# Layer 0 of a four-layer network: score tiles in PSUM banks of their own, single banks for the rest, and two convolutions as matrix products

## The chip, the cores and the metric

The kernel runs on one core of one Trainium2 chip. The metric is the time of one execution on the device in microseconds; the time before is a median of three executions, 4436.91 us (4435.02 to 4451.55). One more execution was profiled. A core has five engines that work side by side: TensorE (PE in the profile, its weight loads PEld), VectorE (DVE), ScalarE (ACT), GpSimd (POOL) and SyncE (SP), which issues most DMAs. TensorE writes into PSUM only, here eight banks of 512 fp32 numbers per partition; ScalarE and VectorE read the banks.

## The reference, cut to what matters

The input is eight samples of 256 channels by 32 x 32 points, fp32. Four layers follow one another. Only layer 0 is touched:

```python
def _attention(x, ...):
    qkv = _bn(_conv1x1(x, qkv_w), ...).reshape(B, NH, 2 * KD + HD, N)     # 4 heads, KD = 32, HD = 64, N = 1024
    attn = softmax(einsum('bhkn,bhkm->bhnm', q, k) * SCALE)
    out = einsum('bhdm,bhnm->bhdn', v, attn).reshape(B, Cc, H, W)
    out = out + _bn(_dwconv3(v_img, pe_w), ...)
    return _bn(_conv1x1(out, proj_w), ...)

def _edffn(x, pi_w, dw_w, fft_p, po_w):
    x = _conv1x1(x, pi_w)                  # 256 -> 1024 channels
    x = _dwconv3(x, dw_w)                  # 3 x 3, each channel by itself
    x1, x2 = x[:, :hid], x[:, hid:]
    x = gelu(x1) * x2
    x = _conv1x1(x, po_w)                  # 512 -> 256
    # patches of 8 x 8: rfft2, times fft_p, irfft2
    ...

x = x + gamma1 * _attention(_ln(x, norm1_w, norm1_b), ...)
x = x + gamma2 * _edffn(_ln(x, norm2_w, norm2_b), ...)
```

Layers 1 to 3 (a deformable convolution; an attention with a routed feed-forward; an attention with a mixture of experts) read what layer 0 wrote.

## The kernel before, in words

`fast0` is layer 0. It is written as generators: each `yield` ends a piece, and `by_time` merges the pieces of all streams by a time of their own, given at the end of `fast0` in units of half an attention step (`T = 32` units to a sample). The merged order is a priority; a planner then orders the instructions of each engine, by this priority and by when its own costs say that inputs and buffers are there. The order it finds is fixed in the program, each engine runs its list in order, and semaphores hold an instruction until its inputs and buffers are ready. Work of layer 1 (`net.head()`, and what follows it) is merged in behind layer 0's end, and the planner may place it earlier where an engine would be idle.

The streams of a sample `b`:

- `before_attention`: root-mean-square norm (`normed`: squares, `ms` as a product with `mean64`, `r`, then `rb`, which spreads `r` over the partitions, and `xn` = x times `rb` on VectorE), the products for v, q and k (`projected`), the transposes of v (`vT`), and the 3 x 3 position convolution (`pe`), for which `thrice` holds three shifted copies of v, loaded by DMA.
- `attention`: one stream for all samples, 8 x 2 x 8 = 128 steps. A step makes scores for four heads (`s`, four products of 512 columns, L1357), two exponentials of 1024 on ScalarE (`e`, L1363), and for the step before it the sums of `e` on VectorE (L1319) and the products with v (`A`, L1323). `finish` divides by the sums (`D`, `rr`, `av`), adds `o`, and makes the output product (`proj`), which VectorE adds to x (L1351).
- `before_gates` and `gates`: the second norm, then eight convolutions `convolved(i)` in the order 0, 1, 4, 5, 2, 3, 6, 7. Each is a product (`pi`, L78), its reading by ScalarE (`hp`, L1398), and `depthwise`: the middle tap on ScalarE (L1223) and eight taps on VectorE (L1230), each a multiply-add over the image. `hp` has two buffers. GELU and a product on VectorE (`gate`, L1409) follow, and `gated` goes to DRAM.
- `transforms`: four groups of patches: `po` (L1448), its copy `u` by ScalarE, the forward transform (`fwd`, L1455), a product with `gain` on VectorE (L1456), the transform back (`back`, L1463) and an addition to x on VectorE (L1469).

PSUM: `psS` has three pairs of banks for all tiles of `pair` and `bank`, scores among them; `psA` has one pair for `A`. `bank` takes a pair too and uses its first half. When the attention stream is done, `att.close()` gives up its buffers, and the rest of layer 0 (the last sample's gates, the transforms of the last two) runs with the head of layer 1, which has two banks of its own.

Of the kernel before, what the change touches and what calls it, by code (L numbers as in the profile page):

```python
# [17 lines left out]
P = 128  # L18
B = 8
# [1074 lines left out]
def fast0(net, io):  # L1094
    tc, nc = net.tc, net.nc
    NH, KD = 4, 32
    SCALE = KD ** (-0.5)
    NT = N // P
    yield HOLD
    with ExitStack() as ctx, ExitStack() as att:  # L1100
        wp = io.pool(ctx, "f0w", 1)
        one = io.pool(ctx, "f0a", 1)
        two = io.pool(ctx, "f0b", 2)
        five = io.pool(ctx, "f0e", 5)
        psS = io.pool(ctx, "f0s", 3, PSUM)

        awp = io.pool(att, "f0aw", 1)
        aone = io.pool(att, "f0aa", 1)
        atwo = io.pool(att, "f0ab", 2)
        afive = io.pool(att, "f0ae", 5)  # L1110
        psA = io.pool(att, "f0am", 1, PSUM)
        nc.scalar.preload_act_table_set("natural_log_exp_and_others")

        vec = net.load(wp, "f0_vec")
# [18 lines left out]
        pib = wp.tile([P, 8], F32, name="pib")  # L1133
        gain = net.load(wp, "l0_gam2")

        def pair(name):
            return psS.tile([P, 2, HF], F32, tag="S", name=name)

        def bank(name):
            return pair(name)[:, 0]  # L1140

        with ExitStack() as tmp:
            ini = io.pool(tmp, "f0i", 1)
# [54 lines left out]
        def normed(xn, x, sq):  # L1198

            ps = bank("ms")  # L1200
            for k in range(KC):
                s_ = sq(k)
                nc.scalar.activation(s_, x[:, k, :], AF.Square)
                for h in range(2):
                    nc.tensor.matmul(
                        ps[64 * h : 64 * h + 64], lhsT=net.mean64, rhs=s_[:, bass.ts(h, HF)],
                        start=(k == 0), stop=(k == KC - 1),
                    )
            r = one.tile([P, HF], F32, tag="r", name="r")
            net.rsqrt(r, ps, net.eps6)  # L1210
            yield
            pr = pair("rb")
            for h in range(2):
                nc.tensor.matmul(
                    pr[:, h], lhsT=net.unit[64 * h : 64 * h + 1, :], rhs=r[64 * h : 64 * h + 1, :],
                    start=True, stop=True,
                )
            pr = pr.rearrange("p h n -> p (h n)").unsqueeze(1).to_broadcast([P, KC, N])
            nc.vector.tensor_tensor(xn, x, pr, ALU.mult)  # L1219

        def depthwise(out, src, taps):

            nc.scalar.activation(out, src, AF.Identity, scale=taps(4))  # L1223
            for t_ in (0, 1, 2, 3, 5, 6, 7, 8):
# [6 lines left out]
                if t_ % 2:  # L1231
                    yield

        def before_attention(b):
            xn = aone.tile([P, KC, N], F32, tag="xn", name="xn")
            nc.sync.dma_start(out=xn, in_=io.src[b])
            yield
            v = aone.tile([P, KC, N], F32, tag="v", name="v")
            yield from normed(xn, xn, lambda k: v[:, k, :])
            yield  # L1240
            def projected(d, w, j, norm):
                ps = pair("qkv")
                for h in range(2):
                    net.linear(ps[:, h], w, xn, bass.ts(j, P), bass.ts(h, HF))
                nc.scalar.activation(d, ps.rearrange("p h n -> p (h n)"), AF.Identity, scale=sc(norm), bias=sh(norm))

            for c in range(KC):
                projected(v[:, c, :], wv, c, 2 + c)
                yield
            for d, (j, name) in ((qs, (0, "q")), (ks, (1, "k"))):  # L1250
                d[b] = atwo.tile([P, N], F32, tag=name, name=name)
                projected(d[b], wqk, j, j)
                yield

            va = vas[b] = atwo.tile([P, NT, KC, P], F32, tag="va", name="va")
            for t4 in range(0, NT, 4):
                ps = pair("vT")
                for i in range(4):
                    for c in range(KC):
                        lo = (i % 2) * C + c * P  # L1260
                        nc.tensor.transpose(ps[:, i // 2, lo : lo + P], v[:, c, bass.ts(t4 + i, P)], net.ident)
                nc.scalar.copy(
                    va[:, t4 : t4 + 4].rearrange("p t c d -> p (t c d)"), ps.rearrange("p h n -> p (h n)")
                )
                yield

            o = os[b] = atwo.tile([P, KC, N], F32, tag="o", name="o")
            for c in range(KC):
                ps = pair("pe")
                for h in range(2):  # L1270

                    thrice = aone.tile([96, 4, HF], F32, tag="thrice", name="thrice")
                    edge = thrice[0:32, :, :IMG] if h == 0 else thrice[64:96, :, HF - IMG :]
                    nc.gpsimd.memset(edge, 0.0)  # L1274
                    for j in range(3):
                        n = HF * h + IMG * (j - 1)
                        lo, hi = max(0, n), min(N, n + HF)
                        for g in range(4):
                            nc.sync.dma_start(
                                out=thrice[32 * j : 32 * j + 32, g, lo - n : hi - n],  # L1280
                                in_=v[32 * g : 32 * g + 32, c, lo:hi],
                            )
                    yield
                    for j, s_ in enumerate((0, -1, 1)):
                        for g in range(4):
                            to, fr = (
                                img(a)[:, :, max(0, -d_) : IMG - max(0, d_)]
                                for a, d_ in ((ps[32 * g : 32 * g + 32, h], s_), (thrice[:, g, :], -s_))
                            )
                            nc.tensor.matmul(  # L1290
                                to, lhsT=wpe[:96, c, s_ + 1, g, :], rhs=fr, start=(j == 0), stop=(j == 2)
                            )
                    yield
                nc.scalar.activation(
                    o[:, c, :], ps.rearrange("p h n -> p (h n)"), AF.Identity, scale=sc(4 + c), bias=sh(4 + c)
                )
                yield

        def attention():
# [31 lines left out]
            def finish(b, gq, A, total, x):  # L1331
# [13 lines left out]
                nc.vector.tensor_tensor(av, av, rr.unsqueeze(1).to_broadcast([P, KC, HF]), ALU.mult)  # L1345
                nc.vector.tensor_tensor(o[:, :, cols], o[:, :, cols], av, ALU.add)
                yield
                ps = pair("proj")
                for c in range(KC):
                    net.linear(ps[:, c], wproj, o, bass.ts(c, P), cols)  # L1350
                    nc.vector.scalar_tensor_tensor(x[:, c], ps[:, c], sh(6 + c), x[:, c], ALU.add, ALU.add)  # L1351
                nc.sync.dma_start(out=mids[b][:, :, cols], in_=x)

            for i, (b, gq, kt) in enumerate(steps):
                ss = [pair("s") for _ in range(2)]
                for h in range(NH):
                    nc.tensor.matmul(  # L1357
                        ss[h // 2][:, h % 2], lhsT=ks[b][32 * h : 32 * h + 32, bass.ts(kt, P)],
# [31 lines left out]
        def gates(b):  # L1390
            xn = xs.pop(b)

            def convolved(i):
                hp = two.tile([P, N], F32, tag="hp", name="hp")
                ps = pair("pi")
                for h in range(2):
                    net.linear(ps[:, h], wpi, xn, bass.ts(i, P), bass.ts(h, HF))
                nc.scalar.activation(hp, ps.rearrange("p h n -> p (h n)"), AF.Identity, bias=pib[:, i : i + 1])  # L1398
                a = cv[i] = five.tile([P, N], F32, tag="a", name="a")
                yield  # L1400
                yield from depthwise(img(a), img(hp), lambda t_: dw_taps[:, i, t_ : t_ + 1])

            cv, sts = {}, {}

# [23 lines left out]
        def transforms(b):  # L1428
# [12 lines left out]
            for pr in range(4):  # L1441
                hc, x = ahead.pop(pr)
                if pr < 3:
                    fetch(pr + 1)
                ps = pair("po")
                for pc in range(2):
                    for k in range(4):
                        nc.tensor.matmul(  # L1448
                            ps[:, 0, bass.ts(pc, C)], lhsT=hc[:, k, pc, :], rhs=wpo[:, k, :],
                            start=(k == 0), stop=(k == 3),  # L1450
                        )
                u = one.tile([P, 2, C], F32, tag="u", name="u")
                nc.scalar.copy(u.rearrange("p t c -> p (t c)"), ps[:, 0])
                yield
                nc.tensor.matmul(ps[:, 1], lhsT=fwd, rhs=u.rearrange("p t c -> p (t c)"), start=True, stop=True)  # L1455
                nc.vector.tensor_tensor(  # L1456
                    u, ps[:, 1].rearrange("p (t c) -> p t c", c=C), gain.unsqueeze(1).to_broadcast([P, 2, C]), ALU.mult
                )
                yield
                back = pair("back")  # L1460
                for c in range(KC):
                    for pc in range(2):
                        nc.tensor.matmul(  # L1463
                            back[:, 0, (2 * c + pc) * P : (2 * c + pc + 1) * P], lhsT=u[:, pc, bass.ts(c, P)],
                            rhs=inv, start=True, stop=True,
                        )
                for c in range(KC):
                    xt = x[:, c, :].rearrange("p (h q w) -> p q h w", q=2, w=16)
                    nc.vector.tensor_tensor(  # L1469
                        xt, back[:, 0, bass.ts(c, C)].rearrange("p (q h w) -> p q h w", q=2, w=16), xt, ALU.add  # L1470
                    )
                nc.sync.dma_start(out=io.dst[b][:, :, bass.ts(pr, C)], in_=x)
                yield
# [13 lines left out]
            next(streams[1][2])  # L1487
        rest = by_time(streams, until=main)
        att.close()
        by_time(rest + [[T * B + 1, 2, net.head()]])  # L1490


# [1657 lines left out]
```

## Time and profile before

| | |
|---|---|
| median of three executions | 4436.91 us (4435.02 to 4451.55) |
| the profiled execution, its span | 4446.59 us, 4444.7 us |
| PE busy over the span | 4017.9 us (90%) |
| DVE, ACT busy over the span | 2316.8 us (52%), 2146.1 us (48%) |
| mean granted TensorE clock | 0.952 |
| one tap of `depthwise` on VectorE (L1230) | 1232 ns, 512 of them |
| `pi`, 128x512 (L78) | 512 records, mean 629 ns |
| scores `s` (L1357), exponentials `e` (L1363) | 1024 records, mean 643 ns; 256, mean 1020 ns |

A product of fp32 numbers shows as two records of TensorE, so `pi` has 8 x 8 x 2 x 2 = 256 products and 512 records. [...]the pitch between records is what counts, 3.70 us for eight of `pi` in a row. "Idle before" is the idle time of an engine ahead of an instruction, and behind the arrow stands what ended it. Views of a stretch of time give microseconds from the start of the span.

### The profile page before, as it was taken

The numbers are of one execution on the slowest core, as the hardware profiler recorded it, in microseconds if no ns is written. First come the engines' busy times: TensorE is split into PE (matmuls) and PEld (weight loads), VectorE is DVE, ScalarE is ACT, GpSimd is POOL, SyncE is SP. The second block draws the span as 40 slices with busy tenths as digits, with TensorE's granted clock in tenths as the row PEclk, the third lists the DMA queues.
The fourth block names the chain that finished last, engine by engine and source line by source line (L and its number), as shares of the span: only waits on it lengthen the run. The fifth ranks groups of instructions, "written<-read, shape, count | busy, mean of one in ns | idle before, by whom it ended". The sixth has DMA issues, their size and how long they took to land. (4 is left out here: it accounts for less than half of the span.)

```text
span 4444.7 us, 52329 instructions
## 1 busy us (share of the span) xinstructions
PE 4017.9 (90%) x19836; PEld 1911.5 (43%) x19836; DVE 2316.8 (52%) x3935; ACT 2146.1 (48%) x2736; POOL 555.6 (13%) x634
## 2 busy tenths in 40 slices
PE   8989999999887899989999978888999999999887
PEld 3223333333333444444444435553333443336776
DVE  2387777777888677742222266622333223324355
ACT  3454445444443466634334364425555555566443
POOL 0000000000000000000000023330000000353753
PEclk9999999999998999999999989999999999999997
DMA  2212222222222111010001023362100000236666
GB/s 85 77 50 83 87 73 88 81 76 80 69 89 82 58 59 49 31 41 19 20 19 38 10 88 105 97 207 76 34 29 29 10 20 29 75 122 201 183 221 244
DMA packets 188423, 348.44 MB, mean 78 GB/s; under 512 B 23706, under 2 KB 132460, under 8 KB 176644
## 3 DMA queue, kind: packets, MB, share of 16 engines
q1 hardware_dynamic: 165396, 293.31, 20.4%
q0 software_dynamic: 19104, 46.45, 3.0%
q10 hardware_dynamic: 3664, 5.24, 0.3%
q8 instruction: 160, 2.62, 0.2%
q14 instruction: 99, 0.81, 0.1%
HBM read 174.24 MB, written 152.04 MB: 73 GB/s over the span
## 5 line engine op out<-in xcount | busy, mean ns | idle before, releaser
L1230 DVE SCALAR_TENSOR_TENSOR a<-hp,w_f_vec,a 128x992 f32<-128x992 f32 (+1 forms) x512 | 627.9, 1232 | 150.2 <-ACT a L1223 142.6
L2611 ACT ACTIVATE e<-s,five 128x1024 f32<-128x1024 f32 x512 | 539.3, 1110 | 274.2 <-PE s L2605 273.7
L2605 PE MATMUL s<-q,k 32*128 32x512 f32 x2048 | 368.5, 673 | 20.0 <-ACT e L2611 17.9
L1363 ACT ACTIVATE e<-s 128x1024 f32<-128x1024 f32 x256 | 249.6, 1020 | 229.0 <-PE s L1357 228.9
L2589 PE MATMUL A<-e,v 128*32 128x512 f32 x2048 | 296.9, 635 | 17.8 <-ACT e L2611 17.8
L1319 DVE TENSOR_TENSOR sum<-sum,e 128x1024 f32<-128x1024 f32 x192 | 230.7, 1219 | 115.9 <-ACT e L1363 115.9
L1323 PE MATMUL A<-e,va 128*32 128x512 f32 x2048 | 288.7, 602 | 0.0
L78 PE MATMUL pi<-xn,w_l_wpi 128*128 128x512 f32 x512 | 248.0, 629 | 36.9 <-ACT e L1363 20.0
L1357 PE MATMUL s<-q,k 32*128 32x512 f32 x1024 | 195.1, 643 | 12.8 <-DVE xn L1219 7.1
L2605 PEld LDWEIGHTS s<-q,k 32*128 32x128 f32 x2048 | 116.7, 191 | 202.5 <-issue 82.8
L1398 ACT ACTIVATE hp<-pi,pib 128x1024 f32<-128x1024 f32 x64 | 71.4, 1115 | 234.6 <-PE pi L78 228.7
L78 PEld LDWEIGHTS pi<-xn,w_l_wpi 128*128 128x128 f32 x512 | 97.8, 200 | 177.9 <-issue 110.4
L1681 PE MATMUL pos<-pos,w_f_sel 64*128 64x512 f32 x576 | 163.7, 633 | 5.4 <-ACT ay L1707 2.1
L2759 PE MATMUL h<-xk,w 128*128 128x128 f32 x1136 | 145.5, 283 | 20.4 <-DVE xk L2747 20.2
L1021 POOL DMA_INDIRECT res<-y,to x142 | 143.5, 1011 | 123.0 <-issue 87.3
L2730 ACT COPY w<-w_l3f_w 128x512 f32 x142 | 88.3, 624 | 144.1 <-PE h L2759 142.3
L2759 PEld LDWEIGHTS h<-xk,w 128*128 128x128 f32 x1136 | 142.1, 198 | 26.9 <-DVE xk L2747 20.2
L78 PE MATMUL h<-xk,w_l2f_w 128*128 128x512 f32 x256 | 125.5, 648 | 27.9 <-DVE xk L2136 27.9
L1274 POOL MEMSET thrice<- 32x128 f32 x32 | 6.3, 196 | 1117.4 <-PE pe L1290 1072.3
L1323 PEld LDWEIGHTS A<-e,va 128*32 128x32 f32 x2048 | 61.3, 109 | 193.8 <-issue 191.5
L2589 PEld LDWEIGHTS A<-e,v 128*32 128x32 f32 x2048 | 42.5, 110 | 234.2 <-issue 201.7
L1021 POOL DMA_INDIRECT so<-xl,rows x128 | 129.5, 1012 | 90.5 <-DMA xl<-mox 62.7
(397 smaller groups left out, 7032.9 us busy)
## 6 DMA issues: line engine op xcount, KB each, us to landing
x<-d SPq DMA_DIRECT2D x32, 1024.0 KB
xs<-so SPq DMA_DIRECT2D x70, 260.0 KB
so<-zero SPq DMA_DIRECT2D x5, 3380.0 KB
thrice<-v SPq DMA_DIRECT2D x256, 64.0 KB
gated<-st SPq DMA_DIRECT2D x32, 512.0 KB
hc<-gated SPq DMA_DIRECT2D x32, 512.0 KB
d<-x SPq DMA_DIRECT2D x16, 1024.0 KB
xl<-mox SPq DMA_DIRECT2D x64, 256.0 KB
```

What stands on the lines that cost most here:

```text
L78: self.nc.tensor.matmul(ps, lhsT=w[:, i, m], rhs=src[:, i, cols], start=(i == 0), stop=(i == k - 1))
L1021: made = self.nc.gpsimd.indirect_dma_start(**args)
L1230: nc.vector.scalar_tensor_tensor(to, fr, taps(t_), to, ALU.mult, ALU.add)
L1319: nc.vector.tensor_tensor(half, half, e[j], ALU.add)
L1323: nc.tensor.matmul(state["A"][32 * h : 32 * h + 32, c, :], lhsT=vas[b][:, kt, c, 32 * h : 32 * h + 32], rhs=e[h // 2][:, h % 2, :], start= ...
L1357: nc.tensor.matmul(ss[h // 2][:, h % 2], lhsT=ks[b][32 * h : 32 * h + 32, bass.ts(kt, P)], rhs=qs[b][32 * h : 32 * h + 32, bass.ts(gq, HF) ...
L1363: nc.scalar.activation(es[i][j], ss[j], AF.Exp, scale=SCALE)
L1681: nc.tensor.matmul(ps[:, bass.ts(h, HF)], lhsT=sel[r, t, xy, :], rhs=poss[b][r, :], start=True, stop=True)
L2589: nc.tensor.matmul(A[32 * h : 32 * h + 32], lhsT=v[:, kt, c * P + 32 * h : c * P + 32 * h + 32], rhs=e[:, h, :], start=first, stop=last,)
L2605: nc.tensor.matmul(ss[h // 2][:, h % 2], lhsT=k[32 * h : 32 * h + 32, c, bass.ts(kt, P)], rhs=q[32 * h : 32 * h + 32, c, bass.ts(hh, HF)], ...
L2611: nc.scalar.activation(e[:, 2 * j : 2 * j + 2], ss[j], AF.Square, scale=SCALE, bias=five)
L2759: nc.tensor.matmul(ps[:, j, m], lhsT=ws[j][:, k, bass.ts(m, P)], rhs=xk[:, j, k], start=(k == 0), stop=(k == KC - 1),)
```

## The change

- `psS` now has two pairs, and only scores use it. All other tiles take single banks `X`, of which there are two while attention runs: 4 + 2 + 2 (`psA`) is again eight. Tiles that were a pair (`pi`, `qkv`, `vT`, `pe`, `rb`, `proj`) become two banks, and ScalarE or VectorE reads each bank by an instruction of its own. `po` and `fwd`, which shared a pair, are two tiles. The tile of `pe` is taken after `thrice` is loaded, not before.
- After the attention stream `X` is a new pool of four banks.
- For the last sample, convolutions 1 and 7 go through `by_products`: ScalarE makes nine 128 x 128 matrices with the taps of a channel on the diagonal, and for each half of the image nine products with shifted windows add up in a bank, which ScalarE copies out.

```diff
+    BY_PRODUCTS, HROWS = (1, 7), IMG // 2
...
-        psS = io.pool(ctx, "f0s", 3, PSUM)
+        own = {"X": io.pool(ctx, "f0x", 2, PSUM)}
...
-        psA = io.pool(att, "f0am", 1, PSUM)
+        psS, psA = io.pool(att, "f0s", 2, PSUM), io.pool(att, "f0am", 1, PSUM)
...
-        def pair(name):
-            return psS.tile([P, 2, HF], F32, tag="S", name=name)
-
         def bank(name):
-            return pair(name)[:, 0]
+            return own["X"].tile([P, HF], F32, tag="X", name=name)
...
+        def by_products(out, src, i):
+
+            diag = own["diag"].tile([P, 9, P], F32, tag="dg", name="dg")
+            for t_ in range(9):
+                nc.scalar.activation(diag[:, t_], net.ident, AF.Identity, scale=dw_taps[:, i, t_ : t_ + 1])
+            for h in range(2):
+                ps = bank("dw")
+                for n, t_ in enumerate((4, 0, 1, 2, 3, 5, 6, 7, 8)):
+                    dy, dx = t_ // 3 - 1, t_ % 3 - 1
+                    lo, hi = max(0, HROWS * h + dy) - dy, min(IMG, HROWS * h + HROWS + dy) - dy
+                    x0, x1 = max(0, -dx), IMG - max(0, dx)
+                    nc.tensor.matmul(
+                        img(ps)[:, lo - HROWS * h : hi - HROWS * h, x0:x1], lhsT=diag[:, t_],
+                        rhs=img(src)[:, lo + dy : hi + dy, x0 + dx : x1 + dx], start=(n == 0), stop=(n == 8),
+                    )
+                    if n in (4, 8):
+                        yield
+                nc.scalar.copy(out[:, bass.ts(h, HF)], ps)
...
             def projected(d, w, j, norm):
-                ps = pair("qkv")
                 for h in range(2):
-                    net.linear(ps[:, h], w, xn, bass.ts(j, P), bass.ts(h, HF))
-                nc.scalar.activation(d, ps.rearrange("p h n -> p (h n)"), AF.Identity, scale=sc(norm), bias=sh(norm))
+                    ps = bank("qkv")
+                    net.linear(ps, w, xn, bass.ts(j, P), bass.ts(h, HF))
+                    nc.scalar.activation(d[:, bass.ts(h, HF)], ps, AF.Identity, scale=sc(norm), bias=sh(norm))
...
-                ps = pair("proj")
                 for c in range(KC):
-                    net.linear(ps[:, c], wproj, o, bass.ts(c, P), cols)
-                    nc.vector.scalar_tensor_tensor(x[:, c], ps[:, c], sh(6 + c), x[:, c], ALU.add, ALU.add)
+                    ps = bank("proj")
+                    net.linear(ps, wproj, o, bass.ts(c, P), cols)
+                    nc.vector.scalar_tensor_tensor(x[:, c], ps, sh(6 + c), x[:, c], ALU.add, ALU.add)
...
-                ss = [pair("s") for _ in range(2)]
+                ss = [psS.tile([P, 2, HF], F32, tag="S", name="s") for _ in range(2)]
...
-                ps = pair("pi")
                 for h in range(2):
-                    net.linear(ps[:, h], wpi, xn, bass.ts(i, P), bass.ts(h, HF))
-                nc.scalar.activation(hp, ps.rearrange("p h n -> p (h n)"), AF.Identity, bias=pib[:, i : i + 1])
+                    ps = bank("pi")
+                    net.linear(ps, wpi, xn, bass.ts(i, P), bass.ts(h, HF))
+                    nc.scalar.activation(hp[:, bass.ts(h, HF)], ps, AF.Identity, bias=pib[:, i : i + 1])
...
-                yield from depthwise(img(a), img(hp), lambda t_: dw_taps[:, i, t_ : t_ + 1])
+                if b == B - 1 and i in BY_PRODUCTS:
+                    yield from by_products(a, hp, i)
+                else:
+                    yield from depthwise(img(a), img(hp), lambda t_: dw_taps[:, i, t_ : t_ + 1])
...
         att.close()
+        own["X"], own["diag"] = io.pool(ctx, "f0t", 4, PSUM), io.pool(ctx, "f0d", 2)
```

`rb`, `vT`, `pe`, `po`, `fwd` and `back` are changed in the same way as `projected` and `proj`.

## The prediction

> **What bounds the kernel now.** I read the page's slices first, then a table of stretches, then the waits of the engine that is busiest in them, then the order of time where the stretches change. The slices (slice 12 ends at 1333 us) put layer 0 in the first 13: from the third on TensorE is at 80 to 90% and VectorE at 70 to 80%, and in slices 11 to 13 TensorE falls and VectorE rises.
>
> ```profile
> PE   8989999999887899989999978888999999999887
> DVE  2387777777888677742222266622333223324355
> ```
>
> The table of stretches, cut where the timeline shows attention's last step (1310), the last sample's normalised input (1358), its last convolution (1462) and layer 1's first `pos` product (1501):
>
> ```profile
> core 0: us, PE busy (x) PEld busy (x) DVE busy (x) ACT busy (x) POOL busy (x), PEclk, DMA share, GB/s
> 50.00:1310.00 1260.00, 1151.51 (x5644) 417.54 (x5641) 915.62 (x846) 589.42 (x629) 6.07 (x31) 0.97 0.24 74
> 1310.00:1358.00 48.00, 27.48 (x74) 9.89 (x74) 32.72 (x39) 16.10 (x23) 6.01 (x6) 0.69 0.46 168
> 1358.00:1462.00 104.00, 69.70 (x248) 35.40 (x244) 95.99 (x107) 34.89 (x43) 0.00 (x0) 0.86 0.18 62
> 1462.00:1501.00 39.00, 38.58 (x174) 21.52 (x168) 10.03 (x19) 4.74 (x9) 0.50 (x2) 0.97 0.36 116
> ```
>
> Up to 1310 TensorE sets the pace (1151.5 of 1260 us; idle 108.5). From 1358 VectorE does (96.0 of 104; TensorE idle 34.3). From 1462 TensorE is full again. What ends TensorE's idle time in 50 to 1310:
>
> ```profile
> PE pi L78 <- ACT e L1363: 20.0, 18, 1.1
> PE proj L78 <- DVE x L1351: 15.5, 9, 2.5
> PE pi L78 <- DVE xn L1219: 13.6, 7, 2.2
> PE qkv L78 <- DVE xc L1469: 9.3, 4, 2.3
> PE pe L1290 <- DMA thrice<-v: 9.1, 7, 2.1
> PE proj L78 <- ACT e L1363: 7.8, 7, 1.1
> PE s L1357 <- DVE xn L1219: 7.1, 5, 5.7
> PE proj L78 <- DVE o L1346: 5.4, 2, 4.2
> ...
> PE s L1357 <- ACT e L1363: 2.2, 2, 1.1
> ...
> PE s L1357 <- DVE u L1456: 1.5, 1, 1.5
> PE s L1357 <- DVE xc L1469: 1.2, 1, 1.2
> ```
>
> `pi` doesn't read `e`, and `s` reads none of `xn`, `u`, `xc`: these are waits for a pair of banks, not for data. The tail in order of time, VectorE's and TensorE's:
>
> ```profile
> 1411.07 11.57 DVE L1230 SCALAR_TENSOR_TENSOR a<-hp,w_f_vec,a 128x992 f32<-128x992 f32 x10
> ...
> 1447.46 0.58 PE L1548 MATMUL gn_m<-gn_mv,w_f_gsel 128*128 128x1 f32 x2 [11.48 <-DVE gn_mv L1545]
> 1456.02 0.59 PE L1557 MATMUL gn_v<-gn_t,w_f_gsel 128*128 128x1 f32 x2 [7.97 <-DVE gn_t L1554]
> ```
>
> VectorE adds one tap every 1.157 us, back to back, and TensorE has nothing to do for 20 us.
>
> [...]18 waits of `pi` for an exponential, none over 1.1 us. [...]the rows show 586 (`u`) and 1010 (`av`). [...]So the bank of an operation queued behind taps stays taken. `back` shows it: from its last matmul to the start of a reading addition 4.2 us pass on average, against 0.04 us (median) from `pi` to `hp`, which ScalarE reads.
>
> **The change part by part.**
>
> *Scores of their own.* The 30.0 us of waits for an exponential (20.0 + 7.8 + 2.2) go, since nothing but scores waits for `e` any more, and a step's scores have TensorE's 1.9 us of values and some 6 us of other work before they are needed again. The scores' 9.8 us behind VectorE (7.1 + 1.5 + 1.2) go too.
>
> *All else in two single banks.* `proj` behind `x` and `qkv` behind `xc` (24.8 us) were waits for a tile that VectorE empties late. Its queue is as full as before, so I let a third go (8.3): `proj`'s second product no longer shares a tile with the first's reader.
>
> *New waits.* I followed each use in 300 to 1200 us from its first matmul to its last reader's end, double ones cut in two. A third is open for 62 us of 900, mostly with one of `u`, `xn` or `xc` pending. Over 1260 us that is 87 us if TensorE finds nothing else to do, and 0 if it always does. Of the 62, 26 come from `pe`, which held its pair while `thrice` was loaded and now takes a bank after the load; leaving these out, 51. Values and scores can fill about 3 of every 10 us, and the planner can reorder. I take 15. Behind a waiting product stand the next step's scores, for which ScalarE waits 229 us already, so ScalarE would have room to catch up but TensorE would not.
>
> *Smaller tiles.* ScalarE reads 64 `hp`, 32 `qkv`, 16 `vT` and 16 `pe` tiles in two: 128 more instructions, each 2 x 0.586 - 1.010 = 0.162 us, so 21 us. ScalarE is busy 589 of 1260 us and idles 191 us ahead of `hp` alone: hidden; uncovered it would cost the 21. `rb` in halves: 16 x (2 x 1.22 - 2.28) = 2.6 us of VectorE, hidden behind TensorE. The other way, `pi` may start when half of `xn` is there: 14 products of `xn` in the stretch save up to 1.1 us each, of the 13.6 listed; I take 4. `pe`'s moved allocation moves no DMA. `po` and `fwd` in two banks, `back` and `D` in one: as many instructions, nothing.
>
> Sum to 1310: -30.0 - 9.8 - 8.3 - 4 + 15 = -37 us.
>
> *Two convolutions on TensorE.* Removed from VectorE: 2 x 8 taps x 1.157 = 18.5 us; from ScalarE two first taps, 2.3 us. Added to TensorE: over nine windows a half has 512 + 2 x 496 (own rows), 480 + 2 x 465 (clipped) and 512 + 2 x 496 (unclipped) columns, 4418 in all or 8.63 full products. A full one is two records at the 0.43 us pitch of `pi` (8 in 3.70 us[...]). 2 x 2 x 8.63 x 0.86 = 29.7 us. Weight loads of 0.19 us hide under records of 0.43. Added to ScalarE: 18 diagonals, which the trace doesn't show: between the 0.22 us of a 64x32 copy and the 0.37 of a 128x256 one[...], and four copies of 0.59, 2.4 us. ScalarE is busy 35 of 104 us: hidden; uncovered up to 8.
>
> In 1358 to 1462 TensorE then has 69.7 + 29.7 = 99.4 us to do and VectorE 96.0 - 18.5 = 77.5. TensorE becomes the bound, with 5 us of gaps 104: as long as before. Of its work there 9.6 us (`z` 6.6, `z8` 1.1, `c` 1.9) is layer 1's and can slip, so convolution 7 may end by 1452, its gate, its store and the four transforms of the last sample following. But the slipped 9.6 us then fall into the stretch that is full (38.6 of 39). So I put the tail at 0, between -18.5 (VectorE stays the bound and TensorE's gaps take it all) and +10 (the products delay `pi` and the transforms behind them on the same queue). A product waiting for its diagonal stops those too.
>
> Total -37. The profiled execution took 4446.6 us (span 4444.7, 1.9 around it) and lies 9.7 above the median of 4436.9; I take the difference from the median: 4400.
>
> **The rivals.**
> 1. *Mine*: waits for exponentials go, tail even: 4400. Chance 0.50.
> 2. *VectorE bounds the tail after all*: 20 us of empty TensorE ahead of 1461 speak for it, the 99 us of work against. -37 - 18.5: 4381. With fewer new waits (0 for 15), 4366. Chance 0.22.
> 3. *No gain*: what two banks cost is what the third pair cost, or the layers behind take up the slack. For it: 65 us of the 108.5 idle would have to be replaced, while two uses suffice for 93% of the time. About 4435. Chance 0.14.
> 4. *Slower, the ring of two banks becomes the bound*: one bank held behind VectorE's taps (`back` 5.0 us per use on average, `u` 4.2) leaves one, and each half of `pi` then waits for its own reading, about 1 us. All 87 us come: -52 + 87 = +35, so 4472. It decides from 52 us of new waits on, more than half of the 87. For it: VectorE busy 916 of 1260. Against: `pi`, `qkv`, `vT`, `pe`, most of the uses, are read by ScalarE within 0.1 us. Chance 0.14.
>
> **How the numbers follow.** 0.5% is 22 us, about what a measurement of this kernel can tell from no change. Case 1 runs from 4378 to 4425, a tenth of it above 4415; faster: 0.45 + 0.21 = 0.66. Same: 0.05 + 0.01 + 0.12 + 0.04 = 0.22. Slower: 0.02 + 0.10 = 0.12. The range from 4362 (case 2 with no new waits, 4 lower) to 4446 takes in case 3 and leaves out most of case 4 and a few hundredths below. Without case 4 and 3: 4366 to 4425.
>
> **What would show it.** Right: attention's last step near 1275; no `pi` or `proj` behind `e`; `s` behind `e` alone; TensorE's idle time up to there near 70 us; waits for `hp`, `x`, `u`, `xc` on the order of 30 us; 72 new records of `dw` in two runs of 15 us; 16 fewer taps; `pos` of layer 1 37 us earlier, with the stretch from xn to `pos` as long as now. Wrong: `pi`, `qkv` or `back` behind `u`, `xc`, `xn` for over 50 us (case 4), or convolution 7's gate 15 us earlier after its xn than now (case 2), or a different order in layers 1 to 3, which this working takes as unchanged.

## The result, and the profile after

The kernel after takes 4428.6 us (median of 15 executions, 4416.34 to 4442.28) against 4442.94 us for the kernel before (15 executions beside it), a ratio of 0.997 [0.9959, 0.998] (in brackets, here and below, the 95% interval): 14 us, 0.3%, where 37 us were forecast. The profiled execution took 4437.04 us (before: 4446.59), its span is 4435.3.

The page's slices, busy share of TensorE and VectorE in fortieths of the span:

```profile
PE   8989999999878989989999978888999999999887
DVE  2387887887886677742222266622333223324345
```

The picture is the old one; the difference lies in the stretches. The table of stretches of the kernel after, cut at its own marks (attention's last step 1279, the last sample's xn 1326, its last gate 1434, layer 1's first `pos` 1477):

```profile
core 0: us, PE busy (x) PEld busy (x) DVE busy (x) ACT busy (x) POOL busy (x), PEclk, DMA share, GB/s
50.00:1279.00 1229.00, 1139.77 (x5639) 423.81 (x5640) 920.42 (x862) 618.52 (x740) 6.08 (x31) 0.95 0.24 76
1279.00:1326.00 47.00, 30.21 (x83) 9.78 (x73) 34.40 (x43) 22.70 (x43) 6.01 (x6) 0.72 0.57 205
1326.00:1434.00 108.00, 96.96 (x285) 47.23 (x284) 69.79 (x74) 33.88 (x46) 0.00 (x0) 0.93 0.13 45
1434.00:1477.00 43.00, 39.80 (x178) 22.61 (x178) 11.86 (x29) 5.59 (x12) 0.50 (x2) 0.92 0.34 113
```

Attention ends 30 us earlier (1309.4, now 1279.1). From xn to the last gate 108.3 us pass where 102.3 did, and from there to `pos` 43.3 where 39.7 did. VectorE has 26 us less to do from xn to the gate (95.99 before, 69.79 now), and the stretch is longer all the same; TensorE is busy for 97 of the 108. The waits of TensorE up to 1279:

```profile
PE pi L78 <- DVE xc L1491: 28.9, 11, 4.5
PE proj L78 <- DVE o L1364: 11.0, 6, 4.4
PE pi L78 <- DVE xn L1217: 7.8, 1, 7.8
PE pe L1308 <- DMA thrice<-v: 7.7, 5, 2.1
...
PE fwd L1477 <- DVE x L1369: 4.6, 6, 0.8
PE proj L78 <- ACT st L1441: 4.5, 1, 4.5
PE qkv L78 <- DVE xc L1491: 4.0, 4, 1.0
PE fwd L1477 <- DVE xn L1217: 3.2, 4, 1.5
...
PE proj L78 <- ACT e L1381: 2.2, 2, 1.1
```

The 20.0 us of `pi` behind an exponential are gone. In their place `pi` waits 28.9 us for `xc`, which it doesn't read: for a bank that `back` holds until VectorE has added it.

Three quantities say more about attention than waits alone: TensorE's idle time, its busy time at full clock, and what half clock took from it. "Half clock" names the stretches in which the profile's record grants TensorE a clock of 0.5; half of TensorE's busy time in them counts as lost (the records of `pi` start 429 ns apart at full clock and 853 ns apart in these stretches, medians of the kernel after). From 50 us to attention's last step:

| | length | idle | busy at full clock | lost to half clock |
|---|---|---|---|---|
| before | 1259.4 | 108.5 | 1112.6 | 38.3 |
| after | 1229.1 | 89.2 | 1081.7 | 58.2 |
| difference | -30.3 | -19.3 | -30.9 | +19.9 |

The whole: attention -30.3, the tail up to `pos` +7.0 (191.3, now 198.3), the rest of layer 1 up to its last `acc` +7.4 (419.9, now 427.3), from there to the first `xk` of a later layer +5.3, of which 2.3 is lost to half clock, and +1.3 behind: -9.3, the difference of the two spans. (The tail is what lies between attention's last step and the first `pos`; "layer 1" below is the stretch from there to the last `acc`.)

### The profile page after: what moved, and what is told of

It reads as the page before. It is cut to its first block, busy times and chain, and to the rows that moved or that the text cites. A ratio compares the mean times of both kernels' runs of the same rounds, so it can differ in the third digit from the quotient of the medians.

```text
span 4435.3 us, 52682 instructions
## 1 busy us (share of the span) xinstructions
PE 4047.8 (91%) x19908; PEld 1937.0 (44%) x19908; DVE 2301.6 (52%) x3935; ACT 2184.9 (49%) x2884; POOL 554.4 (13%) x634
## 5 line engine op out<-in xcount | busy, mean ns | idle before, releaser
L1230 DVE SCALAR_TENSOR_TENSOR a<-hp,w_f_vec,a 128x961 f32<-128x961 f32 (+1 forms) x496 | 608.9, 1233 | 147.0 <-ACT a L1223 138.9
L2612 PE MATMUL A<-e,v 128*32 128x512 f32 x2048 | 296.4, 634 | 18.5 <-ACT e L2634 18.5
L78 PE MATMUL pi<-xn,w_l_wpi 128*128 128x512 f32 x512 | 266.3, 662 | 39.1 <-DVE xc L1491 28.9
L1416 ACT ACTIVATE hp<-pi,pib 128x512 f32<-128x512 f32 x128 | 87.5, 687 | 202.7 <-PE pi L78 197.5
```

Source lines behind the costliest of these rows:

```text
L78: self.nc.tensor.matmul(ps, lhsT=w[:, i, m], rhs=src[:, i, cols], start=(i == 0), stop=(i == k - 1))
L1230: nc.vector.scalar_tensor_tensor(to, fr, taps(t_), to, ALU.mult, ALU.add)
L2612: nc.tensor.matmul(A[32 * h : 32 * h + 32], lhsT=v[:, kt, c * P + 32 * h : c * P + 32 * h + 32], rhs=e[:, h, :], start=first, stop=last,)
```

## The experiments

Ratios are to the kernel before on the same chip; where its median was 4475 or 4480 us, the chip is a slower one, and only ratios are compared across chips.

### Which part brings the gain

`banks_only` is the kernel after with the old convolutions, `products_only` the kernel before with the two convolutions as products (`dw` takes one of the shared pairs), and `after_again` the kernel after once more.

```diff
-    BY_PRODUCTS, HROWS = (1, 7), IMG // 2
+    BY_PRODUCTS, HROWS = (), IMG // 2          # banks_only
+    BY_PRODUCTS, HROWS = (1,), IMG // 2        # one_product
+    BY_PRODUCTS, HROWS = (7,), IMG // 2        # seven_only
```

> The changed kernel without its convolutions by products: all eight of the last sample go through VectorE. Theory A (the banks gave the 30 us by which attention ended earlier, and the products of convolution 7 stand alone at the end and cost the tail some 7 us): attention ends near 1279 us again, the way from there to the first pos of layer 1 takes 190 us, not 198, and the time is 4420 us, ratio 0.995. Theory B (the products carry the gain and the banks are even): attention's end moves back towards 1300 or the tail grows by 15 us, and the time is 4440 us or more, ratio 0.999 to 1.003.

> The kernel before, its three shared pairs kept, with convolutions 1 and 7 of the last sample by products. Theory A: attention ends near 1309 us as before, the tail grows from 191 to 198 us, the time is 4449 us against 4442, ratio 1.001 to 1.002, and VectorE stands idle for 14 us ahead of the last gate. Theory B: the tail shrinks by 10 to 18 us, ratio 0.996 to 0.998.

> The changed kernel once more, beside the others of this group, for a second profile of it. Theory D (the half-clock windows of TensorE differ from execution to execution of the same program): at full clock attention takes 1214 to 1221 us again (its length less the clock lost in it), while the lost clock in attention lies anywhere from 45 to 65 us; ratio 0.996 to 0.998. Theory E (the program itself fixes them): 64.8 us lost again, attention ends at 1279.

Measured: `banks_only` 0.9936 [0.9918, 0.9953], `products_only` 1.0054 [1.0039, 1.0069], `after_again` 0.9964 [0.995, 0.9978]. The banks carry the whole gain, 28 us of 4475, and the products cost: 0.003 beside the new banks, some 13 us, and 24 us beside the old ones. Theory B falls, and Theory A's cost of the products, 7 us, was too low: in `products_only` the tail takes 209.8 us, not 198. In `after_again` attention has 1081.1 us of busy time at full clock, as `after` (1081.7), 93.5 of idle time (89.2) and 49.6 lost (58.2): so work and order are fixed, and the loss to half clock differs by some 9 us between two executions. From the start of the span, with half of every half-clock stretch taken off, attention ends at 1214.2 and 1219.5 us, as Theory D has it.

### What the two convolutions cost, and where

> The changed kernel with convolution 1 alone by products; 7 goes through VectorE. Theory A: the products of convolution 1 run beside VectorE and save it 9 us, TensorE has 15 us less to do than with two, and nothing of TensorE's stands alone at the end: from attention's end to pos 185 us, time 4415 us, ratio 0.994. Theory B (each product pays): between the changed kernel and banks_only, ratio 0.998 or so.

> After, with convolution 7 alone as products, convolution 1 on VectorE. Theory G (each convolution as products costs TensorE 15 us in a stretch that it fills, and gives VectorE 9): half of what both cost, a ratio near 0.9953. Theory J (convolution 7 stands alone at the end, where its 15 us of products take the place of 9 us of taps with nothing beside them, so it costs all): near 0.997, as after, with xn to the last gate 6 to 8 us longer than with the banks alone (99.9). Theory K (the other one costs all): near 0.9936, as the banks alone.

Measured: 0.9956 [0.9943, 0.997] and 0.9936 [0.9918, 0.9953], so one would say that convolution 1 costs everything. (In `one_product` the tail takes 198.9 us, not 185: its Theory A falls.) But half-clock stretches lay differently in these executions (42.2 us lost in attention in one, 53.0 in the other). So the four cases were run again in a form with fewer of these stretches (the section "Half clock" below says how). `rb_64_rows` there has both convolutions as products; these three have none, 1 and 7:

> The new banks without products, the spreading of r from 64 rows. Theory H: as much gain from the rows as after had, 0.9936 less 0.005, near 0.989; attention with 17 half-clock windows or fewer. Reference for the next two.

> The same with convolution 1 alone as products. Theory K (convolution 1 carries the cost, because transforms and the next product stand behind its 15 us on TensorE's queue while VectorE waits): 8 to 15 us more than without products, a ratio 0.002 to 0.0035 higher, xn to the last gate near 108. Theory G (half each): 7 us more, 0.0016 higher.

> The same with convolution 7 alone as products. Theory K: as without products, within 0.001, xn to the last gate near 101. Theory G: 0.0016 higher. Theory J (convolution 7 carries the cost): 0.003 higher, xn to the last gate 107.

Measured: 0.9894 [0.9867, 0.9921], 0.9899 [0.9876, 0.9922], 0.9904 [0.9882, 0.9927], medians 4397.2, 4400.5 and 4400.2 us. `rb_64_rows` ran on another chip. Times alone can't part 3 us from 6. The stretches of the profiles can:

| products | xn to last gate | tail | TensorE busy in the tail, at full clock | TensorE idle in the tail | layer 1 | tail + layer 1 |
|---|---|---|---|---|---|---|
| none | 100.4 | 189.8 | 125.8 | 43.5 | 419.5 | 609.3 |
| 1 | 108.2 | 198.9 | 140.8 | 37.4 | 416.8 | 615.7 |
| 7 | 101.1 | 191.0 | 135.6 | 37.1 | 424.2 | 615.2 |
| 1 and 7 | 107.9 | 197.9 | 150.3 | 31.1 | 422.4 | 620.3 |

Each costs 6 us and both 11 (with one row in `rb`: 609.3, 618.6, 614.5 and 625.6, so 9, 5 and 16; the tail of `after_again`, 198.3 us, equals that of `after`). With TensorE's loss to half clock taken off these sums, the two groups agree better: 7 us for convolution 1, 3.5 to 5 for 7, some 14 for both. So neither carries all of the cost: J and K fall, and Theory G holds in the main. This rests on one profile of each kernel. Each adds 15 us of products to TensorE, and only 6 of these go into time in which it stood idle. Convolution 1 lengthens the tail; 7 pushes 22 of 64 `z` records of layer 1 past the first `pos`, and layer 1 pays. The waits of VectorE from xn to the gate, without products:

```profile
DVE a L1232 <- ACT a L1225: 7.3, 2, 6.0
```

with convolution 1 as products:

```profile
DVE xc L1493 <- PE back L1487: 12.9, 1, 12.9
```

and with convolution 7:

```profile
DVE st L1432 <- ACT a L1253: 14.6, 1, 14.6
```

One wait each, as long as the products. The order of time in the kernel after shows both:

```profile
1336.44 4.22 PE L1245 MATMUL dw<-hp,dg 128*128 128x512 f32 x10
...
1342.53 7.73 PE L1245 MATMUL dw<-hp,dg 128*128 128x496 f32 x18
1350.19 1.92 PE L1619 MATMUL off<-xpad,w_f_woff 64*32 64x512 f32 x16
1352.04 3.46 PE L1245 MATMUL dw<-hp,dg 128*128 128x496 f32 x8
1355.34 0.83 PE L1485 MATMUL back<-w_l_inv,u 128*128 128x128 f32 x6
...
1412.99 2.07 PE L1644 MATMUL z<-w_f_wdef,xd 64*128 64x512 f32 x2 [8.77 <-DVE z L1648]
1414.99 17.12 PE L1245 MATMUL dw<-hp,dg 128*128 128x512 f32 x36
```

`back` stands behind the products of convolution 1 on TensorE's queue, and VectorE, whose next instruction is the addition of `back`, waits until 1356. Convolution 7's `hp` is read by ScalarE only at 1413.7, behind the GELU of convolution 3, for which VectorE's taps had to end; TensorE stands idle 8.8 us ahead of that (the wait ends with VectorE's copy of a `z`), then its products run for 17.1 us (at a granted clock of 0.88), and after the first 3.5 us of them nothing is left to do on VectorE beside them.

Could convolution 1 be put where `back` doesn't wait for it? `one_reordered` takes the last sample's convolutions in the order 0, 4, 1:

```diff
+                for i in (0, 4, 1) if b == B - 1 and j == 0 else (j, j + 1, 4 + j):
+                    yield from convolved(i)
```

> one_product with the last sample's convolutions in the order 0, 4, 1 in place of 0, 1, 4, so the pi that VectorE needs next is ahead of the products on TensorE's queue. Theory F (VectorE starves because pi of convolution 4 and back stand behind 15 us of products): the 12.9 us wait for back and most of the 6 us wait after it go, VectorE waits some 5 us for pi of convolution 5 in their place, from xn to the last gate 100 us, not 108, the time 8 us below one_product, ratio 0.994. Theory G (TensorE has too much to do, wherever the products stand): 107 us or more, ratio 0.9955.

Measured: 0.9946 [0.9929, 0.9962], xn to the last gate 107.9 as with the old order. VectorE's waits there begin with

```profile
DVE u L1477 <- PE fwd L1476: 12.9, 2, 12.2
```

The wait for `back` has become one for `fwd`. Theory F's remedy fails: in both orders something that VectorE needs next stands behind 15 us of products. Products cut into smaller pieces between other work, or given a later place in the merged order, were not tried.

### The late reader of a bank

In `back_by_act` ScalarE copies `back` to SBUF, and VectorE adds from there; `banks_back` is the same without products. (To make room, two constants that are used at the start share the new buffer; those lines are left out.)

```diff
+                bs = one.tile([P, HF], F32, tag="bs", name="bs")
+                nc.scalar.copy(bs, back)
-                        xt, back[:, bass.ts(c, C)].rearrange(...), xt, ALU.add
+                        xt, bs[:, bass.ts(c, C)].rearrange(...), xt, ALU.add
```

> The changed kernel, but ScalarE copies back from its bank to SBUF (32 copies of 0.59 us) and VectorE adds from there, so the bank doesn't wait for VectorE. Theory A (what is left of TensorE's idle time in attention is above all the bank that VectorE empties late): the 34 us of waits for xc (pi 28.9, qkv 4.0, D 1.1) fall below 6, attention ends near 1255 us, windows at half clock in attention fall from 25 to 18 or fewer since the 4 us gaps ahead of them are gone, time 4403 us, ratio 0.991. Theory C (the next late reader of VectorE's, x or u, takes over, or ScalarE's queue does): attention ends at 1270 or later, ratio above 0.995.

> The two edits that ran faster, together: no convolution by products, and ScalarE empties back. Theory A (they lie in different stretches, so they add): attention ends near 1251 us, from there to pos 190 us, layer 1 takes 420, ratio 0.990. Theory C (the gain of one is used up by the other): ratio 0.993 as for each alone.

Measured: 0.9936 [0.9922, 0.995], where `after` has 0.997 and 0.9964, and 0.9902 [0.9887, 0.9918]. In `back_by_act` attention ends at 1251.0, as Theory A has it, but its tail and layer 1 take 631.8 us together (625.6 in `after`), 22 half-clock stretches remain, not 18, and the ratio lies between the two theories. The waits of TensorE up to there in `banks_back`:

```profile
PE fwd L1479 <- DVE xn L1219: 18.1, 4, 4.5
PE proj L78 <- DVE o L1366: 17.7, 8, 4.4
```

No wait for `xc` remains, which confirms that `back` held the bank; of its 34 us in the kernel after, 15 came back as more waits of `fwd` and 7 as more of `proj` behind `o` (theory C: the next late readers take over). TensorE's idle time is 82.1 us where `banks_only` has 91.6, and the two edits add, as Theory A of `banks_back` has it (0.990).

`proj` waits for `o`, which VectorE makes late. `banks_back_pool` has GpSimd make `av` and `o`:

```diff
-                nc.vector.tensor_tensor(av, av, rr..., ALU.mult)
-                nc.vector.tensor_tensor(o[:, :, cols], o[:, :, cols], av, ALU.add)
+                nc.gpsimd.tensor_tensor(av, av, rr..., ALU.mult)
+                nc.gpsimd.tensor_tensor(o[:, :, cols], o[:, :, cols], av, ALU.add)
```

> banks_back with the two operations av and o of attention (L1345 and L1346 of the kernel before, 32 of 1.22 us) on GpSimd, which has nothing to do in layer 0. Theory A (what is left is VectorE's queue, in which o stands behind taps): the waits of proj for o (21.7 us) fall to a few us, VectorE gets 39 us less to do, attention ends near 1235 us, ratio 0.987. Theory H (GpSimd needs longer for the two than VectorE's queue did, 3 us each or more): proj waits for o as long or longer, ratio as banks_back.

Measured: 0.9988 [0.9975, 1.0001], attention's end at 1303.1. The wait of `proj` has grown:

```profile
PE proj L78 <- POOL o L1366: 36.6, 15, 6.3
```

GpSimd is too slow for it (theory H of that expectation): `av` takes 3.10 us there and `o` 3.21 (medians), 1.22 each on VectorE in `banks_back`. And more than that: VectorE's sums of exponentials in `banks_back_pool` (mean of one in ns behind the busy time), up to 1250 us:

```profile
L1335 DVE TENSOR_TENSOR sum<-e 128x1024 f32<-128x1024 f32 x31 | 65.5, 2119 | 53.7 <-ACT e L1383 25.9 <-PE D L1358 22.5 <-ACT v L1266 5.3
```

took 1219 ns each in `banks_back`, where VectorE makes `av` and `o`. Half clock took 60.8 us from attention, for 44.1; that is one profile each.

### Scores of their own, or single banks

`one_pair` is the kernel before with two pairs for scores and one pair for all else.

```diff
-        psS = io.pool(ctx, "f0s", 3, PSUM)
+        own = {"X": io.pool(ctx, "f0x", 1, PSUM)}
+        psS, psA = io.pool(att, "f0s", 2, PSUM), io.pool(att, "f0am", 1, PSUM)
-            return psS.tile([P, 2, HF], F32, tag="S", name=name)
+            return own["X"].tile([P, 2, HF], F32, tag="X", name=name)
```

> Before, with two pairs for scores alone and one pair for everything else (two pairs after attention): scores have banks of their own, but the rest isn't split into single banks. Prediction's sum: the 30 us of waits for exponentials and the 9.8 of scores behind VectorE go here too; but every tile of the rest waits for the reader of the one before, 64 pi tiles x about 1 us and 16 products of proj, 64 of back behind VectorE: 80 to 110 us of new waits, attention 40 to 70 us longer, a ratio of 1.01 to 1.016. Rival: the planner fills these with scores and values, and the pair is enough: 0.993 to 0.998, as after; then the single banks add nothing.

Measured: 1.0447 [1.0422, 1.0472], 4683.3 us against 4480.6: three times the most that was expected, and for another reason. Attention takes 218 us longer, with only 22 of idle time; TensorE's busy time at full clock is 1268.4 for 1112.6, and half clock took 79.2 for 38.3. Groups of TensorE from 50 to 1527 us, `one_pair`:

```profile
L1323 PE MATMUL A<-e,va 128*32 128x512 f32 x2044 | 357.9, 627 | 0.2
L1357 PE MATMUL s<-q,k 32*128 32x512 f32 x1024 | 316.6, 665 | 22.8 <-ACT e L1363 22.8
```

and before, from 50 to 1300 us:

```profile
L1323 PE MATMUL A<-e,va 128*32 128x512 f32 x2016 | 284.8, 602 | 0.0
L1357 PE MATMUL s<-q,k 32*128 32x512 f32 x1024 | 195.1, 643 | 12.8 <-DVE xn L1219 7.1 <-ACT e L1363 2.2 <-DVE u L1456 1.5
```

The same scores keep TensorE busy 122 us longer (103 us at full clock). They use 32 rows (32*128 in the trace, where `pi` has 128*128), and four that follow one another take no longer than two. The order of time, `one_pair`:

```profile
609.91 1.13 PE L1357 MATMUL s<-q,k 32*128 32x512 f32 x4
610.97 3.70 PE L78 MATMUL pi<-xn,w_l_wpi 128*128 128x512 f32 x8
614.60 1.13 PE L1357 MATMUL s<-q,k 32*128 32x512 f32 x4
```

and before:

```profile
616.70 1.14 PE L1357 MATMUL s<-q,k 32*128 32x512 f32 x8
```

Four records take as long as eight: the order has pulled a step's scores apart. (A product is two records, so it is 1.13 us for two products and 1.14 for four; the four products of `pi`, with as many columns, take 3.70.) The 1024 records of scores come in 267 runs for 154. So banks of their own for the scores are no gain with one pair for all else; in the kernel after, with two single banks, they are. The kernel after differs from `one_pair` in one more thing: `one_pair` still takes the pair of `pe` before `thrice` is loaded, and `pe` waits 28.3 us for it where before has 9.1. Which of the two pulls the order apart was not varied, nor was the later tile of `pe` tried alone in the kernel before. But `one_pair` shows the term that the prediction didn't have: the same effect, the other way round, is in the kernel after. Counting TensorE's time at full clock by the tile that it goes to, from 50 us to attention's end: `A` 270.9, now 255.0; `s` 174.2, now 159.8; `pe` 104.6, now 96.8; `rb` 13.7, now 18.8. (The order is read from single profiles; it is fixed in the program.) A step's 16 products of `A` take 1.92 us in one run, and 1.90 + 1.06 when cut in 10 and 6; of 128 steps, 84 have their products of `A` in one run of 16 before (six more in runs of 32), 107 after; for scores in one run of 8 it is 101 and 107, though the rest of the scores lies in somewhat more pieces (154 runs in all, now 163).

### Half clock

Half-clock stretches in attention last 3.41 us or whole multiples of it. In before, all 11 full-clock windows of that length (on the grid of these stretches) with 2 us or more of idle TensorE are followed by a half-clock one, and none of 253 with under 0.3 us. In the kernel after it is 16 of 16 and 5 of 266; the five, and two more with under 1 us of idle time, all hold `rb`. (Between 1 and 2 us it is 8 of 37 in before.) Three windows in a row of the kernel after:

```profile
core 0: us, PE busy (x) PEld busy (x) DVE busy (x) ACT busy (x) POOL busy (x), PEclk, DMA share, GB/s
1019.75:1023.17 3.42, 3.42 (x16) 0.86 (x12) 3.42 (x4) 1.63 (x3) 0.00 (x0) 1.00 0.00 0
1023.17:1026.58 3.41, 3.32 (x15) 1.40 (x14) 3.38 (x5) 1.63 (x3) 0.00 (x0) 1.00 0.11 42
1026.58:1029.99 3.41, 3.37 (x4) 1.51 (x5) 3.39 (x3) 1.06 (x2) 0.00 (x0) 0.50 0.43 162
```

In the second TensorE is busy for 3.32 of 3.41 us, and the third gets half the clock. The second holds four `rb`, six `s` and four `vT`. `rb` multiplies one row of ones with one row of `r`. `rb_64_rows`, the kernel after but for this, makes the same numbers from 64 equal rows:

```diff
+        self.unit64 = self.const.tile([P, P], F32, name="unit64")
+        nc.gpsimd.memset(self.unit64, 1.0 / 64)
...
-                    pr, lhsT=net.unit[64 * h : 64 * h + 1, :], rhs=r[64 * h : 64 * h + 1, :], start=True, stop=True
+                    pr, lhsT=net.unit64[64 * h : 64 * h + 64, :], rhs=r[64 * h : 64 * h + 64, :], start=True, stop=True
```

`banks_back_rb64` does it to `banks_back`, and `before_rb64` to the kernel before; these two read one column of 1/64 128 times in place of a matrix. The three kernels without products, with 1 and with 7 above have the form shown.

> After, with the spreading of r made from 64 equal rows with weights of 1/64 in place of one row with weights of 1; the columns, the results and the time of a product at full clock stay. Theory H (a stretch of one-row products, scores on 32 rows and transposes counts as little work, and the next window of 3.4 us gets half the clock): the 3 to 5 half-clock windows of attention that follow a window without idle time go, 20 or 21 windows in place of 25, 5 to 8 us less clock lost, a ratio 0.0015 lower than after's, near 0.995. Theory I (these windows have another cause, such as a short idle time that the trace doesn't show): as many half-clock windows and the same time as after, near 0.9965.

> The new banks without the two products, with the transform back copied out by ScalarE, and the spreading of r made from 64 rows (weights 1/64). Theory H: 4395, a ratio of 0.9885, and 17 or 18 half-clock windows in place of 21. Theory I: as without the change of rows, 0.990.

> Before, with the spreading of r from 64 rows (weights 1/64), nothing else. If the change brought the low-row windows in (they stand beside scores and transposes after it, beside products of 128 rows before it): 2 or 3 half-clock windows fewer, 5 us or less, a ratio of 0.9985 to 1.0. If before had lost as much by them: near 0.995, as after gained by it.

Measured: 0.9917 [0.99, 0.9934] (0.997 and 0.9964 with one row), 0.9863 [0.9845, 0.9882] (0.9902 with one row), and 0.9983 [0.9974, 0.9992]. A window of `rb_64_rows` with four `rb` and six `s`, and the next:

```profile
846.88:850.29 3.41, 3.41 (x14) 1.27 (x13) 3.38 (x5) 0.79 (x2) 0.00 (x0) 1.00 0.19 77
850.29:853.71 3.42, 3.42 (x10) 1.46 (x10) 3.14 (x3) 2.42 (x3) 0.00 (x0) 1.00 0.45 150
```

The clock stays at 1.00. Half-clock stretches in attention: 25 in after, 17 in `rb_64_rows`; none of its 276 windows with under 0.3 us of idle time is followed by one, and of 13 windows that hold two or more `rb` one is, where it was 9 of 15. Busy time at full clock is hardly changed (1081.7, now 1084.7), the loss is 33.9 us for 58.2 (49.6 in `after_again`). Theory H holds, and the gain was underestimated. (Rows and weights were changed together; which of the two counts was not separated.) With the 64 rows, before has 13 such stretches for 19 and loses 23.8 us for 38.3, more than the first case of its expectation says. But with one row none of its windows with `rb` and under 1 us of idle time was followed by half clock; what fell are windows with 1 to 2 us of idle time (8 of 37, then 2 of 37). So how much of this is the rows and how much differs between executions is open. In time before gains 0.0017, after 0.005. By these ratios 0.003 (some 15 us, give or take half of it) of the clock lost to these products came with the change. With 64 rows in both, the change is worth 0.9917 / 0.9983 = 0.9934, and without products 0.9894 / 0.9983 = 0.9911.

`banks_back_rb64` has the lowest ratio of this study: 4421.6 us where before took 4480.6.

## Why the prediction was wrong

4400 us were predicted and 4428.6 measured, inside the range of 4362 to 4446, but the gain is 14 us and not 37, and so below the 22 us that the prediction took for the least that a measurement can tell. By its steps:

- **Scores of their own.** Right: `pi` and `proj` wait 2.2 us for an exponential where they waited 27.8, and `s` for nothing.
- **New waits, 15.** Mis-sized. The mechanism was named with the tile (`back`, read behind taps), and it is there, but waits for `xc`, `u`, `x` in attention come to 41.6 us (28.9 + 4.0 + 1.1 for `xc`, 4.6 + 1.2 for `x`, 1.8 for `u`). Of these 4.0 are left of the old 24.8, where the sum left 16.5; 37.6 are new, where the sum has 15. `proj` also waits longer for `o` (5.4, now 11.0) and once for `st` (4.5). Idle time fell by 19.3 us, not by 37. The sign set for Rival 4, over 50 us of `pi`, `qkv` or `back` behind `u`, `xc` or `xn`, stands at 44.6, where before has 25.1 for the same; but attention became shorter, not 35 us longer. One reading under this term was off: in before 2.0 us pass on average from the last product of `back` to its first addition and 3.4 to its second, not 4.2 (a use of 5.0 us is right), so the wait behind taps was there, but smaller than written.
- **A term that was missing on the good side.** The sum counted idle time alone. In the new order fewer steps are cut in pieces, and TensorE's busy time at full clock fell by 30.9 us.
- **A term that was missing on the bad side.** The granted clock was not in the sum. In the profiles attention lost 19.9 us more to it, in time some 15 of these come from `rb`, as the runs with 64 rows suggest. That attention's total, -30.3, lies near the -37 is luck: idle time gave 19.3 us, and the two missing terms, -30.9 and +19.9, the other 11.0.
- **"So I put the tail at 0."** This step failed, and it decides the miss: tail and layer 1 took 14.4 us more (7.0 and 7.4) where the sum has 0. With the 5.3 us up to `xk` that is what brings attention's -30.3 down to -10.6 there. Products are of the size worked out (15.4 us for convolution 1, 17.1 at a clock of 0.88 for 7, against 14.85 each), diagonals a little dearer (386 ns, against 0.22 to 0.37; that all of it costs ScalarE up to 8 us was an estimate). The step set two sums of work against each other, 99.4 us for TensorE and 77.5 for VectorE, and took the larger with 5 us of gaps. But the two engines feed each other in order: while 15 us of products run, VectorE's next instruction waits for a transform behind them (12.9 us) or for the products themselves (14.3), and TensorE later waits for VectorE. 97 us of TensorE's work took 108, not the 104 of 99.4 with 5 of gaps. The slip of `z` was foreseen, and that it would be paid for at once; it is paid for in layer 1. The runs with and without products put the two together at +11 to +16, just past the +10 that was the upper bound. Rival 2 (-18.5) fell: convolution 7's gate comes 6 us later after xn than before, not 15 earlier.
- **Smaller tiles.** Mis-sized but hidden, as foreseen: the extra for halves was worked out from plain copies (586 ns for 512, 1010 for 1024, so 0.162 us). The mean `hp` takes 687 ns for 512 where 1116 was for 1024, 0.26 us more for two halves, and `v` 778 where 1206 was, 0.35 more.
- **What would show it.** Attention's last step near 1275: 1279.1 and 1274.1 in two executions. TensorE's idle time near 70: 89.2. `pos` 37 us earlier: 23.5, the stretch from xn to it 9.5 longer. 72 records of `dw`: found, one of the two runs cut in three. The layers behind gave nothing back; they lost some more to half clock.

## What to carry to other kernels

Put work on an emptier engine only after looking at what stands behind it on that engine's queue: here 15 us of products made the engine that they were to relieve wait for 13. When banks are dealt out anew, count three things on TensorE and not idle time alone: idle time, how often small products that are quicker in one run are cut apart (here 1.14 us for eight records of scores in one run, 1.13 for four), and the clock granted to what is left (here 58.2 us of attention lost to half clock, and 38.3 before). A product that only spreads a row costs nearly the same with 64 rows as with one (0.5 to 5 us more in some 1100 of TensorE's time here), and with 64 the clock stayed up after 12 of 13 windows that hold two or more of these records (6 of 15 with one row).

## What was not expected of the hardware

- The clock fell after some windows of 3.41 us in which TensorE was busy for 97% and more and which held products of one row, mostly beside products of 32 rows and transposes (5 of 266 in the kernel after); with 64 rows in place of one it didn't (0 of 276). It fell after each window with 2 us or more of idle time in its 3.41 (11 of 11 before, 16 of 16 after); in these five there was next to none (0.11 us at most). What exactly is counted stays open; `s` and `vT` alone were not varied.
- GpSimd took 3.10 us (median; 2.35 the shortest) for a product of two 128x1024 fp32 tiles that takes VectorE 1.22, and VectorE's sums beside it went from 1219 to 2119 ns, its taps from 1233 to 1300. Why the sums slow down so much more than the taps was not shown.
- Two executions of one kernel differ by 9 us of half clock in attention alone (58.2 and 49.6), with the same instructions in the same order. A difference of under 10 us in attention between single profiles says nothing.
